# An adaLN transformer block on one core: the rebuilt end of the program against the plain one

## The chip, the cores and the metric

The kernel runs on one core of one Trainium2 chip. A core has TensorE (PE, matrix products into PSUM), VectorE (DVE), ScalarE (ACT), GpSimd (POOL) and SyncE (SP), which here issues nearly all DMA transfers. Each engine works through its own queue in order; semaphores tie the queues together. The metric is the device time of the whole program in microseconds: the median of several runs. The profile is one execution of the same program.

## The reference

One block of a transformer with adaptive layer norm, on 8 sequences of 1024 tokens, width 512, 16 heads of 32, hidden width 2048, all in f32:

```python
mod = silu(condition) @ Wada + bada
sh_a, sc_a, gt_a, sh_m, sc_m, gt_m = split(mod, 6)
xm = layernorm(x, g1, be1) * (1 + sc_a) + sh_a
x  = x + gt_a * (causal_attention(xm, Wqkv) @ Wproj + bproj)     # softmax over the keys
xm = layernorm(x, g2, be2) * (1 + sc_m) + sh_m
x  = x + gt_m * (gelu(xm @ W1 + b1) @ W2 + b2)
```

The second layer norm needs a token's whole projected row, and the projection needs all 16 heads of that token. So behind the last attention group there is a fixed order: quotient, projection, residual, layer norm, MLP, store.

## The kernel before, in words

**Tiling.** The tokens are cut into 16 blocks of 512 (`NB`), two for each sequence; block n is the first or second half of its sequence. Widths are cut into chunks of 128 (`NC` = 4 for 512). The 16 heads are worked in 4 groups of 4 heads, because four heads of 32 fill 128 partitions. A block is also four tiles of 128 tokens (`NTT`).

**Two streams.** `attend` walks over blocks and groups and issues the attention: for each unit of keys the transposed scores (`weights_T`, line 1456), ACT's exponential into a tile `pT` (L1479, one of three slots), POOL's causal mask for diagonal units (L1484), the product with the values (`weigh`, L1507), and the running sum of the exponentials over the units, by which the output is divided at the end (L1608, L1611). A group of a second-half block has seven units: four of 512 keys by queries, then the diagonal ones of 512, 384 + 128 and 256. Unit 0's `pT` is the accumulator and units 1 to 6 are added to it, four heads each. A slot comes free when its addition and its product are done, so the exponential of unit k waits for the addition of unit k - 2. Everything else (q, k, v, projection, MLP: "linear work") is a generator that yields before each product. PE gets pieces of it between the attention's steps. MLP and projections use Strassen-like schemes with seven products of half size, whose operands are sums such as T3, T4 or `combine`d parts of the hidden tile hT.

**The planner.** The order is written out at build time. `now` holds each engine's planned time, `written` and `left` when a value is there and when its reader is done. `note` adds the cost of each issued instruction. `work` advances the linear thread that can go on soonest, `step_aside` lets linear work go ahead while an attention step would wait. `jobs` are DVE pieces (reciprocals, statistics of the layer norm) that are issued when DVE's planned time isn't ahead of PE's; `pool_jobs` likewise for POOL. `either` puts a two-operand operation on POOL (planned 120 + 2.28 n ns for n elements a partition) or on DVE (60 + 1.24 n), with a margin in favour of POOL:

```python
if max(now["DVE"], t) + on_dve + margin[0] < max(now["POOL"], t) + on_pool:
```

The margin is 1500 ns until `attend` has returned, and 0 from there to the end (L1680).

**A group's end.** `finish` (L1525 on) sums the accumulator over partitions by a product with ones, copies the sums (`rec`) and the outputs (`top`) out on ACT, inverts `rec` in four quarters on DVE (L1540) and multiplies; the result goes into qT's chunk g, which has been used up, and is called `attT` in the projection.
- For most groups the multiplication is one 128x512 operation on POOL (L1557). For group 2 of the last block it is on DVE (L1554).
- For the last group of all, each quarter is multiplied on DVE straight after its reciprocal (L1547) and marked as ready by itself.
- In the last group of all, the additions for heads 1 and 3 are on DVE (L1608), those for heads 0 and 2 on POOL (L1611).

**The projection** (`project_out`, L201 for its products) has 4 chunks for each of 4 tiles. Its result is gated (`y`, L193), added to the residual `xr`, and the bias `gba` is added by pool jobs. For the last block the chunks 0 to 2 of tiles 0 and 1 are issued ahead of the last group's quotient, the chunk 3 of a tile waits for its quarter alone, and each tile is followed by its residual addition (L927) and its own layer norm on DVE and ACT (`normalize_tile`, L596 to L608). Other blocks add to the residual through `either` and normalize all four tiles together (`normalize`, L555 to L580). Then `modulated` transposes on PE (L641) and scales.

**The down projection** (`down`) has four parts. `settle` gates a quarter of the result and adds it to the residual, both through `either` (L158 on DVE, L161 on POOL); `store` writes two tiles out (L988). For the last block the last product is made in two halves of 128 tokens (`last_product`): each half has its own two DVE operations of 128x256 (L1058, L1059) and its own store (L1063).

While the last group of block 15 is worked, the linear work left is the second half of block 14's down projection. It settles the quarters `v_d`, `p_d` and `y_d`.

Of the kernel before, what the change touches and what calls it, by code (L numbers as in the profile page):

```python
# [9 lines left out]
F32 = mybir.dt.float32  # L10
# [12 lines left out]
def kernel(  # L23
# [33 lines left out]
    nc = tc.nc  # L57
# [90 lines left out]
    margin = [1500]  # L148

    def either(out, a, b, op, reads, writes):  # L150

        n = 1
        for d in out.shape[1:]:
            n *= d
        on_dve, on_pool = 60 + 1.24 * n, 120 + 2.28 * n
        t = due(reads, writes)
        if max(now["DVE"], t) + on_dve + margin[0] < max(now["POOL"], t) + on_pool:
            nc.vector.tensor_tensor(out, a, b, op)  # L158
            note("DVE", on_dve, reads, writes, port=True)
# [430 lines left out]
    def normalize_tile(xt, key, t, source):  # L590

        mv = small.tile([P, 2], F32, tag="mv1", name=f"mv_{key}_{t}")
        rstd = small.tile([P, 1], F32, tag="rstd1", name=f"rstd_{key}_{t}")
        offset = small.tile([P, 1], F32, tag="offset1", name=f"offset_{key}_{t}")
        st = small.tile([P, nc.vector.BN_STATS_DIM], F32, tag="st", name=f"st_{key}_{t}")
        nc.vector.bn_stats(st, xt)  # L596
        nc.vector.bn_aggr(mv, st)  # L597
        note("DVE", 850, [source], [("mv", key, t)])
        nc.scalar.activation(rstd, mv[:, 1:2], AF.Sqrt, bias=eps)  # L599
        note_act(300, "sqrt", [("mv", key, t)], [("rstd", key, t)])  # L600
        written["hat", key, t] = NEVER

        def apply():
            nc.vector.reciprocal(rstd, rstd)  # L604
            nc.vector.scalar_tensor_tensor(offset, mv[:, 0:1], -1.0, rstd, ALU.mult, ALU.mult)  # L605
            note("DVE", 360, [("rstd", key, t)], [("rstd", key, t)], port=True)
            xh = tmp.tile([P, D], F32, tag="hat", name=f"xh_{key}_{t}", bufs=NTT)
            nc.scalar.activation(xh, xt, AF.Identity, bias=offset, scale=rstd)  # L608
            note_act(800, None, [("rstd", key, t)], [("hat", key, t)])
            hats.setdefault(key, []).append(xh)  # L610

        return apply

# [52 lines left out]
    def accumulate(pairs, reads=(), close=True):  # L666
        yield reads, [BANK]
        bank = lin_bank()
        for i, (lhsT, rhs) in enumerate(pairs):
            if i:  # L670
                yield [], []
            matmul(banks[bank], lhsT, rhs, i == 0, close and i == len(pairs) - 1, reads, bank)
        return bank
# [213 lines left out]
    def project_out(n):  # L887
        at = take(NC)
        yield [("attended", n)], []
        attT = qTs[n]  # L890
# [16 lines left out]

        for t, xt in enumerate(tiles):
            if last:
                while len(begun) <= max(t, 1):  # L910
                    yield from begin(len(begun))
                bank = begun[t]
                yield [("att", n, t)], []
                matmul(
                    banks[bank], attT[:, NC - 1, ts(t, P)], piece(at[NC - 1]), False, True,
                    [("att", n, t)], bank,
                )
            else:
                bank = yield from accumulate(
                    [(attT[:, c, ts(t, P)], piece(at[c])) for c in range(NC)], [("att", n)]  # L920
                )
# [69 lines left out]
    def down(n, part):  # L991
# [41 lines left out]
        def last_product(u3, next_pieces):  # L1033

            kh, tokens = places["B21"]
            c = half(1, HB)
            gate = gate_rows["gm"][:, c]
            xr = residual[n]
            b, h = blocks[n]
            for m in range(2):  # L1040
                nc.vector.tensor_tensor(u3[:, m, :], u3[:, m, :], gate, ALU.mult)
                nc.vector.tensor_tensor(xr[:, m, c], xr[:, m, c], u3[:, m, :], ALU.add)
                note("DVE", 800, [key("u3")], [("xr", n, m)])
            for m in range(2):
                yield [(n, "B21")], [BANK]
                bank = lin_bank()
                for i in range(NQ):
                    for k in range(2):
                        if i + k:
                            yield [], []  # L1050
                        at_q = 2 * i + k
                        hT = hTs[n, 2 * kh + at_q // NC][:, at_q % NC, tokens]
                        matmul(
                            banks[bank][:, :HB], hT[:, ts(m, P)], halves(next_pieces[i])[:, k, :],
                            at_q == 0, at_q == 2 * NQ - 1, [(n, "B21")], bank,
                        )
                y = tmp.tile([P, HB], F32, tag="y", name=f"y_last_{m}")
                nc.vector.tensor_tensor(y, banks[bank][:, :HB], gate, ALU.mult)  # L1058
                nc.vector.tensor_tensor(xr[:, m, c], xr[:, m, c], y, ALU.add)  # L1059
                note("DVE", 800, [("l", bank)], [("xr", n, m)])  # L1060
                live[bank] = False
                r0 = h * TB + m * P
                nc.sync.dma_start(out[b, r0 : r0 + P, :], xr[:, m, :])  # L1063
            release(*next_pieces)

# [38 lines left out]
        else:  # L1104
# [412 lines left out]
    def finish(n, g):  # L1517
# [25 lines left out]
        if (n, g) == groups[-1]:  # L1543
            for i in range(NTT):
                invert(i)
                some = slice(i * part, (i + 1) * part)
                nc.vector.tensor_tensor(qTs[n][:, g, some], top[:, some], rec[:, some], ALU.mult)  # L1547
                note("DVE", 200, [kr, "top"], [("att", n, i)])
            return

        def quotient():
            invert(3)
            if n == NB - 1 and g == NC - 2:
                nc.vector.tensor_tensor(qTs[n][:, g, :], top, rec, ALU.mult)  # L1554
                note("DVE", 700, [kr, "top"], [("att", n)], port=True)
            else:
                nc.gpsimd.tensor_tensor(qTs[n][:, g, :], top, rec, ALU.mult)  # L1557
# [8 lines left out]
    def attend():  # L1566
        previous = None
        for n in range(NB):
# [21 lines left out]
            for g, k, upto in slots:  # L1590
# [9 lines left out]
                if k > 0:  # L1600
                    acc, first = totals[n, g]
                    for _, c0, w in parts:
                        for j in range(HPG):
                            into = acc[:, j, TB - w :]
                            keys = [("p", slot)], [("acc", n, g), ("p", first)]
                            if j % 2 and (n, g) == groups[-1]:

                                nc.vector.tensor_tensor(into, into, pT[:, j, c0 : c0 + w], ALU.add)  # L1608
                                note("DVE", 150 + 2 * w, *keys, port=True)
                            else:  # L1610
                                nc.gpsimd.tensor_tensor(into, into, pT[:, j, c0 : c0 + w], ALU.add)  # L1611
                                note("POOL", 230 + 2.07 * w, *keys)
# [67 lines left out]
    margin[0] = 0  # L1680
    run_excursions()
    run_jobs(True)
    written["attended", NB - 1] = 0.0
# [51 lines left out]
```

## Time and profile before

| | |
|---|---|
| median of 3 runs | 3650.88 us (3647.89 to 3653.37) |
| the profiled execution | 3647.89 us, its span 3646.2 us |
| mean granted TensorE clock | 0.995 |
| PE busy | 3571.6 us, 98% |
| DVE, POOL, ACT busy | 2179.1, 2014.6, 1329.2 us |
| last addition of the last group | ends at 3520.46 us of the span |
| first product of the last block's MLP | 3545.10 us |
| PE's last product | ends at 3642.13 us |

How to read the lines below: in a timeline a line gives start, duration, engine, line of the kernel, operation, output and inputs, shapes, count, and in brackets how long the engine had been idle before and what released it. `bank` are the three PSUM banks of the linear work. In the windows a line gives the stretch, its length, the busy time of PE, PEld, DVE, ACT and POOL with the number of instructions, then the granted clock, the DMA share and GB/s.

### The profile page before, as it was taken

What the parts mean: (1) busy time and instruction counts of PE and PEld (TensorE: products, weight loads), DVE (VectorE), ACT (ScalarE), POOL (GpSimd) and SP (SyncE); (2) the same over time, 40 slices, a digit from 0 to 9 for tenths busy, and PEclk for the clock granted to TensorE, in tenths of its full rate; (3) what the DMA queues carried; (4) which work ended last, traced back from release to release, by engine and by line L of the source; (5) the groups of instructions that cost most, each with busy time, mean ns of one, the idle gap of its engine ahead of it and who ended that gap; (6) DMA issues with size and microseconds to landing.
All of it is one profiled execution on the core that took longest, in us unless ns stands there. A gap on an engine that the chain in (4) does not pass through costs nothing. (4 is left out here: it accounts for less than half of the span.)

```text
span 3646.2 us, 121167 instructions
## 1 busy us (share of the span) xinstructions
PE 3571.6 (98%) x54821; PEld 1770.1 (49%) x54821; DVE 2179.1 (60%) x2501; ACT 1329.2 (36%) x1413; POOL 2014.6 (55%) x2039
## 2 busy tenths in 40 slices
PE   8999999999999999999999999999999999999999
PEld 4434445445554455544545444454544545445445
DVE  6766675564746557465564656746667465664663
ACT  2335234252333523335242352424524244241431
POOL 3656645656455664566636665456654566544560
PEclk9999999999999999999999999999999999999999
DMA  6623333333333343433434334343333433334334
GB/s 220 225 92 104 104 103 109 123 106 119 114 115 112 106 126 111 134 94 104 126 106 143 91 100 123 106 137 103 97 122 110 140 100 103 117 97 143 92 107 138
DMA packets 307894, 430.35 MB, mean 118 GB/s; under 512 B 25900, under 2 KB 176236, under 8 KB 307380
## 3 DMA queue, kind: packets, MB, share of 16 engines
q1 hardware_dynamic: 307264, 422.56, 37.9%
q8 instruction: 432, 7.08, 0.8%
q14 instruction: 82, 0.67, 0.1%
q10 hardware_dynamic: 116, 0.03, 0.0%
HBM read 394.12 MB, written 28.38 MB: 116 GB/s over the span
## 5 line engine op out<-in xcount | busy, mean ns | idle before, releaser
L1611 POOL TENSOR_TENSOR pT<-pT,pT 128x512 f32<-128x512 f32 (+3 forms) x1266 | 1189.2, 973 | 524.9 <-ACT pT L1479 377.1
L1479 ACT ACTIVATE pT<-st 128x2048 f32<-128x2048 f32 (+1 forms) x320 | 546.5, 1708 | 951.3 <-PE st L1467 909.0
L201 PE MATMUL bank<-w,hT 128*32 128x256 f32 x14336 | 808.6, 380 | 2.8 <-DVE hT L1006 2.1
L1392 DVE TENSOR_REDUCE mx<-sc 128x4 f32<-128x1024 f32 (+3 forms) x381 | 664.4, 1757 | 192.4 <-PE sc L1372 185.8
L201 PEld LDWEIGHTS bank<-w,hT 128*32 128x32 f32 x14336 | 452.1, 110 | 354.0 <-issue 58.0
L201 PE MATMUL bank<-xm_m,w 128*32 128x256 f32 x8192 | 506.6, 380 | 0.6 <-ACT rec L1531 0.5
L1484 POOL TENSOR_SCALAR_AFFINE_SELECT pT<-pT 128x512 f32<-128x512 f32 x256 | 175.3, 696 | 576.9 <-ACT pT L1479 576.9
L201 PE MATMUL bank<-t_m,w 128*32 128x256 f32 x6144 | 383.2, 380 | 0.9 <-ACT hT L188 0.9
L201 PEld LDWEIGHTS bank<-xm_m,w 128*32 128x32 f32 x8192 | 253.3, 110 | 252.0 <-issue 98.0
L1456 PE MATMUL st<-qT,kT 32*128 32x512 f32 (+3 forms) x3072 | 339.6, 526 | 21.0 <-DVE mx L1392 20.0
L1372 PE MATMUL sc<-kT,qT 32*128 32x256 f32 (+3 forms) x3048 | 340.6, 527 | 2.9 <-DVE mx L1392 1.9
L1384 DVE TENSOR_TENSOR sc<-sc,mask 128x1024 f32<-128x1024 f32 (+1 forms) x191 | 166.7, 873 | 248.5 <-PE sc L1372 225.5
L1507 PE MATMUL po<-pT,v 128*32 128x512 f32 (+3 forms) x3072 | 312.7, 493 | 2.2 <-POOL pT L1484 1.2
L201 PEld LDWEIGHTS bank<-t_m,w 128*32 128x32 f32 x6144 | 191.9, 110 | 175.7 <-issue 54.2
L201 PE MATMUL bank<-xm_a,w 128*32 128x256 f32 x3968 | 243.5, 381 | 0.0
L201 PE MATMUL bank<-w,qT 128*32 128x512 f32 x2048 | 241.1, 597 | 0.4 <-DVE qT L1547 0.2
L1540 DVE RECIPROCAL rec<-rec 128x128 f32<-128x128 f32 x256 | 224.6, 919 | 8.5 <-ACT rec L1531 8.5
L1456 PEld LDWEIGHTS st<-qT,kT 32*128 32x128 f32 x3072 | 128.9, 184 | 182.7 <-issue 57.5
L1372 PEld LDWEIGHTS sc<-kT,qT 32*128 32x128 f32 x3048 | 126.8, 184 | 161.0 <-ACT pT L1479 77.4
L193 DVE TENSOR_TENSOR hT<-bank,u_u 128x512 f32<-128x512 f32 x192 | 130.2, 686 | 120.9 <-PE bank L201 116.7
L201 PE MATMUL bank<-t_a,w 128*32 128x256 f32 x2944 | 187.2, 382 | 0.0
L1479 ACT ACT_TABLE_LOAD x89 | 114.2, 1283 | 189.3 <-PE st L1467 188.6
(205 smaller groups left out, 3589.5 us busy)
## 6 DMA issues: line engine op xcount, KB each, us to landing
w<-in_L_cond_W_dram SPq DMA_DIRECT2D x384, 256.0 KB, 2.9
w<-kept_up_S SPq DMA_DIRECT2D x256, 256.0 KB, 2.6
w<-kept_down_S SPq DMA_DIRECT2D x256, 256.0 KB, 2.7
w<-kept_qkv_S SPq DMA_DIRECT2D x180, 256.0 KB, 3.0
w<-in_L_cond_Wqkv_dram SPq DMA_DIRECT2D x147, 256.0 KB, 3.3
hat<-in_x_dram SPq DMA_DIRECT2D x64, 256.0 KB, 3.2
w<-in_L_cond_Wproj_dram SPq DMA_DIRECT2D x64, 256.0 KB, 3.8
xr<-in_x_dram SPq DMA_DIRECT2D x64, 256.0 KB, 4.2
```

Source lines behind the costliest of these rows:

```text
L193: nc.vector.tensor_tensor(out, src, other, op)
L201: nc.tensor.matmul(ps[r, :], lhsT[:, r], rhs, start=start, stop=stop, skip_group_check=True)
L1372: nc.tensor.matmul(sc[:, j, c0 : c0 + w], qTs[n][r, g, ts(qt, P)], keys_of(n, kh)[r, g, :w], start=True, stop=True, skip_group_check=True,)
L1384: nc.vector.tensor_tensor(diagonal, diagonal, mask[:, :span].unsqueeze(1).to_broadcast([P, HPG, span]), ALU.add,)
L1392: nc.vector.tensor_reduce(mx[:, kh, qt, :], sc[:, :, c0 : c0 + w], axis=AX.X, op=ALU.max)
L1456: nc.tensor.matmul(st[:, j, c0 : c0 + w], kT[r, g, ts(k % NTT, P)], qT[r, g, TB - w :], start=(c0 == 0), stop=False, skip_group_check=True,)
L1479: nc.scalar.activation(pT[:, :, :used], st[:, :, :used], AF.Exp, scale=scale)
L1484: nc.gpsimd.affine_select(diagonal, diagonal, pattern=[[0, HPG], [1, P]], compare_op=ALU.is_ge, fill=0.0, base=0, channel_multiplier=-1,)
L1507: nc.tensor.matmul(po[r, TB - w :], v[:, k % NTT, g * P + j * hd : g * P + (j + 1) * hd], pT[:, j, c0 : c0 + w], start=(k == 0), stop=last ...
L1540: nc.vector.reciprocal(some, some)
L1611: nc.gpsimd.tensor_tensor(into, into, pT[:, j, c0 : c0 + w], ALU.add)
```

## The change

The last group, the last projection and the last down projection are treated like all others. The additions of the last group are all on POOL. The quotient of group 2 of the last block is on POOL. The last quotient is one operation on POOL behind four reciprocals. The projection of the last block begins when that quotient has been issued, tile after tile with all four chunks. The residual additions go through `either` and the four tiles are normalized together behind the last of them. The margin of `either` stays 1500 ns to the end. The last product of the down projection is one product of 256 tokens, added to `u3`, settled through `either` and stored with two transfers. The gated results `y` of the last projection lie in four buffers in place of two.

```diff
-    margin = [1500]
...
-        if max(now["DVE"], t) + on_dve + margin[0] < max(now["POOL"], t) + on_pool:
+        if max(now["DVE"], t) + on_dve + 1500 < max(now["POOL"], t) + on_pool:
...
-    def normalize_tile(xt, key, t, source):
...
-    def accumulate(pairs, reads=(), close=True):
+    def accumulate(pairs, reads=()):
...
     def project_out(n):
...
-        last = n == NB - 1
-        if last:
-            for t in range(NTT):
-                written["att", n, t] = NEVER
-        begun = []
-
-        def begin(t):
-
+        for t, xt in enumerate(tiles):
             bank = yield from accumulate(
-                [(attT[:, c, ts(t, P)], piece(at[c])) for c in range(NC - 1)], [("att", n)], False
+                [(attT[:, c, ts(t, P)], piece(at[c])) for c in range(NC)], [("att", n)]
             )
-            begun.append(bank)
-
-        for t, xt in enumerate(tiles):
-            if last:
-                while len(begun) <= max(t, 1):
-                    yield from begin(len(begun))
-                bank = begun[t]
-                yield [("att", n, t)], []
-                matmul(
-                    banks[bank], attT[:, NC - 1, ts(t, P)], piece(at[NC - 1]), False, True,
-                    [("att", n, t)], bank,
-                )
...
-            y = tmp.tile([P, D], F32, tag="y", name=f"y_{n}_{t}", bufs=2)
-            ky = y_key("proj", True)
+            tag, bufs = ("hat", NTT) if n == NB - 1 else ("y", 2)
+            y = tmp.tile([P, D], F32, tag=tag, name=f"y_{n}_{t}", bufs=bufs)
+            ky = ("y", n, t) if n == NB - 1 else y_key("proj", True)
             combine_out(y, bank, banks[bank], gate_rows["ga"], [("row", "ga")], [ky], ALU.mult)
-            if last:
-                run_pool_jobs(True)
-                nc.vector.tensor_tensor(xt, xt, y, ALU.add)
-                note("DVE", 700, [ky, ("xr", n, t)], [("xr", n, t)], port=True)
-                following = normalize_tile(xt, f"m{n}", t, ("xr", n, t))
-                if t > 0:
-                    pending()
-                pending = following
-            else:
-                add_to(xt, y, [ky], [("xr", n, t)])
-        if last:
-            pending()
+            add_to(xt, y, [ky], [("xr", n, t)])
         release(*at)
         run_pool_jobs(True)
-        if not last:
-            normalize(tiles, f"m{n}", [("xr", n, t) for t in range(NTT)])
+        normalize(tiles, f"m{n}", [("xr", n, t) for t in range(NTT)])
...
-        def last_product(u3, next_pieces):
...
-            if n == NB - 1:
-                yield from last_product(u3, next_pieces=[next(at) for _ in range(NQ)])
-                return
             bank, ps = yield from product("B21")
...
-        if (n, g) == groups[-1]:
-            for i in range(NTT):
-                invert(i)
-                some = slice(i * part, (i + 1) * part)
-                nc.vector.tensor_tensor(qTs[n][:, g, some], top[:, some], rec[:, some], ALU.mult)
-                note("DVE", 200, [kr, "top"], [("att", n, i)])
-            return
-
         def quotient():
             invert(3)
-            if n == NB - 1 and g == NC - 2:
-                nc.vector.tensor_tensor(qTs[n][:, g, :], top, rec, ALU.mult)
-                note("DVE", 700, [kr, "top"], [("att", n)], port=True)
-            else:
-                nc.gpsimd.tensor_tensor(qTs[n][:, g, :], top, rec, ALU.mult)
-                note("POOL", 1285, [kr, "top"], [("att", n)])
+            nc.gpsimd.tensor_tensor(qTs[n][:, g, :], top, rec, ALU.mult)
+            note("POOL", 1285, [kr, "top"], [("att", n)])
...
-                            if j % 2 and (n, g) == groups[-1]:
-
-                                nc.vector.tensor_tensor(into, into, pT[:, j, c0 : c0 + w], ALU.add)
-                                note("DVE", 150 + 2 * w, *keys, port=True)
-                            else:
-                                nc.gpsimd.tensor_tensor(into, into, pT[:, j, c0 : c0 + w], ALU.add)
-                                note("POOL", 230 + 2.07 * w, *keys)
+                            nc.gpsimd.tensor_tensor(into, into, pT[:, j, c0 : c0 + w], ALU.add)
+                            note("POOL", 230 + 2.07 * w, [("p", slot)], [("acc", n, g), ("p", first)])
...
     open_unit = attend()
     alone[0] = True
-    margin[0] = 0
     run_excursions()
-    run_jobs(True)
-    written["attended", NB - 1] = 0.0
     close(*open_unit)
```

More of the change, by code (lines that the diff above doesn't have):

```diff
@@ L588, in normalize @@
             add_job(lambda t=t: statistics(t), [sources[t]], key[0] == "m")
-    def normalize_tile(xt, key, t, source):
[L592 to L612, printed above, removed]
     def modulated(key, gain, shift, b, guards):
@@ L671, in accumulate @@
                 yield [], []
-            matmul(banks[bank], lhsT, rhs, i == 0, close and i == len(pairs) - 1, reads, bank)
+            matmul(banks[bank], lhsT, rhs, i == 0, i == len(pairs) - 1, reads, bank)
         return bank
@@ L889, in project_out @@
         yield [("attended", n)], []
-        attT = qTs[n]
+        attT = qTs.pop(n)
         tiles = [residual[n][:, t, :] for t in range(NTT)]
@@ L908, in project_out @@
-        for t, xt in enumerate(tiles):
-            if last:
-                while len(begun) <= max(t, 1):
-                    yield from begin(len(begun))
-                bank = begun[t]
-                yield [("att", n, t)], []
-                matmul(
-                    banks[bank], attT[:, NC - 1, ts(t, P)], piece(at[NC - 1]), False, True,
-                    [("att", n, t)], bank,
-                )
-            else:
-                bank = yield from accumulate(
-                    [(attT[:, c, ts(t, P)], piece(at[c])) for c in range(NC)], [("att", n)]
-                )
-            y = tmp.tile([P, D], F32, tag="y", name=f"y_{n}_{t}", bufs=2)
-            ky = y_key("proj", True)
-            combine_out(y, bank, banks[bank], gate_rows["ga"], [("row", "ga")], [ky], ALU.mult)
-            if last:
-                run_pool_jobs(True)
-                nc.vector.tensor_tensor(xt, xt, y, ALU.add)
-                note("DVE", 700, [ky, ("xr", n, t)], [("xr", n, t)], port=True)
-                following = normalize_tile(xt, f"m{n}", t, ("xr", n, t))
-                if t > 0:
-                    pending()
-                pending = following
-            else:
-                add_to(xt, y, [ky], [("xr", n, t)])
@@ L1031, in product @@
             return bank, banks[bank].rearrange("p (i n) -> p i n", n=HB)
-        def last_product(u3, next_pieces):
[L1035 to L1064, printed above, removed]
         def stage(kind, tag, bufs=1):
@@ L1604, in attend @@
                             into = acc[:, j, TB - w :]
-                            keys = [("p", slot)], [("acc", n, g), ("p", first)]
-                            if j % 2 and (n, g) == groups[-1]:
-                                nc.vector.tensor_tensor(into, into, pT[:, j, c0 : c0 + w], ALU.add)
-                                note("DVE", 150 + 2 * w, *keys, port=True)
-                            else:
-                                nc.gpsimd.tensor_tensor(into, into, pT[:, j, c0 : c0 + w], ALU.add)
-                                note("POOL", 230 + 2.07 * w, *keys)
+                            nc.gpsimd.tensor_tensor(into, into, pT[:, j, c0 : c0 + w], ALU.add)
+                            note("POOL", 230 + 2.07 * w, [("p", slot)], [("acc", n, g), ("p", first)])
                 previous = (n, g, parts, pT, slot, k == n_slots - 1)
```

## The prediction

> **What bounds the kernel now.** I read the page first, then the chain that ended last, then the last 160 us engine by engine in order of time, and then an earlier stretch of the same loop for undisturbed prices. The page:
>
> ```profile
> PE 3571.6 (98%) x54821; PEld 1770.1 (49%) x54821; DVE 2179.1 (60%) x2501; ACT 1329.2 (36%) x1413; POOL 2014.6 (55%) x2039
> ```
>
> PE is the bound nearly everywhere, so an edit counts only where PE waits. All edits sit behind one point, the first partial-sum addition of the last group (block 15, group 3) at 3491.6 us: up to there the two programs issue the same instructions in the same order. PE's own waits behind it stand in the timelines of PE and POOL:
>
> ```profile
> 3515.91 2.34 PE L201 MATMUL bank<-w,hT 128*32 128x256 f32 x40
> 3519.82 1.31 PE L1525 MATMUL bank<-pT,ones 128*32 128x512 f32 x6 [1.57 <-POOL pT L1611]
> 3526.96 9.12 PE L201 MATMUL bank<-w,qT 128*32 128x512 f32 x80 [0.25 <-DVE qT L1547]
> 3542.14 3.04 PE L641 MATMUL bank<-ident,xh_m 128*128 128x128 f32 x13 [0.23 <-ACT xh_m L608]
> 3545.10 2.01 PE L201 MATMUL bank<-xm_m,w 128*32 128x256 f32 x32
> ...
> 3506.31 3.46 POOL L1611 TENSOR_TENSOR pT<-pT,pT 128x512 f32<-128x512 f32 x2
> 3519.06 1.40 POOL L1611 TENSOR_TENSOR pT<-pT,pT 128x256 f32<-128x256 f32 x2
> ```
>
> PE runs without a hole to 3518.25, waits for POOL's last addition (3519.06 + 1.40 = 3520.46), projects until 3526.96 + 9.12 = 3536.08, and gets its first MLP product at 3545.10. Between 3545.10 and 3642.13 it is full again. So three stretches can be priced: up to POOL's last addition (I call its end T, now 3520.46), T to the first MLP product (now 24.64 us), and the tail behind PE's end at 3642.13. POOL has no gap over 0.1 us from 3491.6 to T, though half of the heads are added on DVE.
>
> Undisturbed prices come from an earlier group of the same shape, where POOL adds all four heads (timeline of POOL), and from the tail:
>
> ```profile
> 3056.31 4.99 POOL L1611 TENSOR_TENSOR pT<-pT,pT 128x512 f32<-128x512 f32 x4
> 3064.31 5.55 POOL L1611 TENSOR_TENSOR pT<-pT,pT 128x384 f32<-128x384 f32 x8
> 3070.54 2.80 POOL L1611 TENSOR_TENSOR pT<-pT,pT 128x256 f32<-128x256 f32 x4
> 3098.19 1.28 POOL L1557 TENSOR_TENSOR qT<-top,rec 128x512 f32<-128x512 f32 x1
> ...
> 3642.16 0.43 DVE L1058 TENSOR_TENSOR y_last<-bank,row_gm 128x256 f32<-128x256 f32 x1 [1.65 <-PE bank L201]
> 3642.62 0.42 DVE L1059 TENSOR_TENSOR xr<-xr,y_last 128x256 f32<-128x256 f32 x1
> ```
>
> A group's unit costs POOL 5.0 us for four 512-wide heads; before, two heads took 3.46 beside DVE's two.
>
> **The change, stretch 1: additions of the last group and the quotient of the one before it.** DVE's half of the additions goes to POOL. From 3491.61 POOL has units 1 to 3 at 4.99 (14.97), unit 4 with its mask at 0.72 + 4.99, unit 5 with two masks at 1.19 + 5.55, unit 6 with its mask at 0.75 + 2.80: 30.97 us. The quotient of group 2 comes back from DVE, 1.28 and 0.03 of gap; its reciprocals now find DVE free, so it is issued behind unit 1's additions and stands in this queue. Sum 32.3. In the same stretch lie the eight SBUF operations that finish block 14's last quarters (three on v_d, three on p_d, two on y_d). The first six ran on POOL at about 1.3 to 1.6. The planner moves one to DVE when POOL's planned end is more than 695 + 1500 - 1287 = 908 ns behind the operands. POOL will be nearly 5 us behind when v_d is ready (u_d ends at 3498.0, units 1 and 2 with the quotient end near 3502.9) and further behind for p_d and y_d, so I put all eight on DVE. There they hinder POOL: four additions took 6.33 us at 3442.17 beside three DVE operations, 1.34 more than 4.99, so 0.45 for each DVE operation. Eight cost 3.6. T becomes 3491.6 + 32.3 + 3.6 = 3527.5: 7.0 us later. Bounds: no hindrance, 3.4 later; all eight left on POOL, where the six of v_d and p_d stand ahead of the last additions at 1.28 and 0.07 of gap (8.1 in place of 3.6, the two of y_d behind them), 11.6 later. I take the value between, since the 0.45 comes from three rows that agree (3506.31 gives 0.48, 3520.42 gives 0.45).
>
> On this the Trainium skill (SBUF — State Buffer, section Who interferes with whom) says that the port pair of DVE and GpSimd is a whole-instruction lock, so that the loser blocks fully. By that each DVE operation of 0.69 us would cost POOL 0.69, T would be another 1.9 us later and the forecast 3668; the rows with 0.45 decide.
>
> The PE work of the stretch is unchanged; it runs out some 5 us before T, and what fills that gap in the new order is nothing.
>
> **Stretch 2: T to the first MLP product.** Removed: the quotient by quarters, two tiles begun on their first three chunks, and the tile-wise layer norm. New chain, by rows of this trace: 0.1 to the ones product, 1.04 for it (3487.20), 0.14 and ACT's copy 0.59 (3488.38), 0.1 and four reciprocals 3.38 (3159.39, x4), 0.08 and POOL's quotient 1.28, 0.1, then PE. Only tile 0's first three chunks are done by then, so 13 of 16 chunk products follow, 0.86 each (60 records, 7.5 products, in 6.62 at 3529.46): 11.2. So far 18.0. Behind it: last y 0.72; statistics of four tiles, all issued behind it, 0.81 apart (3143.13 to 3143.95): 3.25; the last residual addition, now POOL's 1.28, is hidden by the first three of them. Root, reciprocal and offset with gaps 0.1 + 0.30 + 0.05 + 0.38, four normalizations on ACT 2.92 (3162.89, x4), 0.05; the last 13 transposes 3.0 as now. That is 10.8, and 28.8 against 24.64: 4.2 later.
>
> PE's clock adds to it. The windows:
>
> ```profile
> 3538.00:3539.00 1.00, 0.15 (x1) 0.16 (x1) 0.90 (x2) 0.79 (x2) 0.00 (x0) 0.74 0.53 177
> 3539.00:3540.00 1.00, 0.32 (x1) 0.03 (x1) 0.97 (x2) 0.00 (x0) 0.00 (x0) 0.50 0.04 13
> 3545.00:3547.00 2.00, 2.00 (x37) 1.11 (x40) 0.95 (x3) 0.91 (x2) 0.21 (x1) 0.92 0.00 0
> ```
>
> The granted clock (third column from the end) halves some 2.4 us after PE's last long run and is back 3 us after work resumes. PE would idle about 5 us before the last weighing, so the ones product runs at half clock: 1.0 more. A second idle of some 2.6 us stands before the quotient lands. Its cost lies between 0 and 1.5 (three microseconds at half clock); I take 0.7. Stretch 2 is 5.9 later. The Trainium skill (TensorE: Matmul & The Clock Gate, Part 1) puts the idle window at about 3.4 us, free-running; by it the second idle would cost nothing and the forecast would be 3665.3. The 2.4 us of the row are nearer to the idle, so I keep 0.7.
>
> The four gate-bias additions move from beside DVE's chain to POOL behind the quotient, 5.1 us within the 11.2 of projection; with the four residual additions POOL has 10.3 there and is free for the last one. If that cover went, 1.3 would show.
>
> **Stretch 3: the MLP and the tail.** With the margin at 1500 again, combinations of hT go to POOL (about 2.8 each) in place of DVE. B11 is done near 5.6 us after 3617.5 and B21 5.6 behind it, needed at 3628 and 3635: free; without that slack each would cost its overrun. T3 on POOL and T4 on DVE are needed 7 us on, free. The last product now ends all at once: y 0.69, gate and residual on POOL 1.31 and 1.33 with gaps 0.2, so 3.5 behind PE against 3642.62 + 0.42 - 3642.13 = 0.9: 2.6 later. Then SP issues two 256 KB stores back to back instead of one that was left over: one issue of 0.4 at least, one transfer of 0.7 more at most; 0.6. Tail 3.2 later. No other queue of SP moves: the weight loads wait on the same releases.
>
> **Sum.** 7.0 + 5.9 + 3.2 = 16.1 us on the profiled execution: span 3646.2 to 3662.3, its time 3647.89 (1.7 around the span) to 3664.0. The median of the runs stands 3.0 above it, so 3650.88 + 16.1, about 3667.
>
> **The rivals.**
> (a) POOL isn't hindered by DVE and PE's clock holds. For it: PE has small jobs in the gap. Against: three contended rows. T 3.4, stretch 2 4.2, tail 3.2: 10.8 later, 3661.7.
> (b) The planner leaves those eight operations on POOL. T 11.6, the rest as above: 20.7, 3671.6. Against: the backlog worked out above.
> (c) The end hardly matters, within 7.3 us (0.2%, about what a measurement of this kernel can tell). It needs T unmoved, stretch 2 at 4.2 and tail 3.0: 7.2, 3658.1. For it: POOL loses six operations of 1.3 to 1.6 us. Against: POOL's additions and masks alone end at 3522.6.
> (d) Faster, by relief of the shared port alone: in the last group POOL and DVE each run long beside each other (POOL 1.73 for a 512-wide head against 1.25), and the change ends that. It decides from T earlier than 3520.46 - 4.2 - 3.2 = 3513.1, so POOL would have to finish in 21.5 us what its rows price at 31.0. By those it ends in (a); were it true with T at 3512, the time would be 3649.8.
>
> **How the numbers follow.** Main case 0.62 (its own range +13 to +19.5, 3664 to 3670.5), (a) 0.18, (b) 0.13, (c) 0.05, (d) 0.02. The range takes (a) to (b) in, with 2.5 to 3.4 us for the spread of the runs shown (3647.89 to 3653.37): 3659 to 3675. Faster 0.02, same 0.05, slower 0.93.
>
> **What would show it.** POOL's line for the additions holds all four heads, its last end near 3527.5; v_d, p_d and y_d operations on DVE inside that stretch; a ones product of about 2 us; 13 chunk products behind one POOL quotient; first MLP product near 3558; behind PE's end two POOL operations of 1.3. Wrong if T comes before 3523, if statistics run between the tiles, or if the four normalizations start before the projection ends; and wrong altogether if PE shows holes inside the 97 us of the MLP, where I cost the margin's change at nothing.

## The result and the profile after

The changed kernel takes 3665.73 us (median of 5 runs, 3662.55 to 3667.84) against 3650.88 us: +14.9 us, a ratio of 1.0040 with a 95% interval of 1.0026 to 1.0055. Run once more beside other kernels it took 3664.88 against 3649.32 us, +15.6, a ratio of 1.0041 (1.0027 to 1.0055). The forecast was 3667.

The profiled execution took 3667.59 us with a span of 3665.9. The last group on POOL, from its timeline:

```profile
3494.01 4.96 POOL L1497 TENSOR_TENSOR pT<-pT,pT 128x512 f32<-128x512 f32 x4 [2.05 <-ACT pT L1383]
3498.92 1.74 POOL L1449 TENSOR_TENSOR qT<-top,rec 128x512 f32<-128x512 f32 x1
...
3512.10 6.40 POOL L1497 TENSOR_TENSOR pT<-pT,pT 128x512 f32<-128x512 f32 x4
...
3519.65 6.39 POOL L1497 TENSOR_TENSOR pT<-pT,pT 128x384 f32<-128x384 f32 x8
...
3526.71 2.77 POOL L1497 TENSOR_TENSOR pT<-pT,pT 128x256 f32<-128x256 f32 x4
```

All four heads are on POOL, group 2's quotient stands behind unit 1, and POOL is busy from the first addition at 3494.01 to the last one's end at 3529.48. Unit 4 takes 6.40 us in place of the undisturbed 4.99, for DVE works beside it (timeline of DVE):

```profile
3512.79 1.65 DVE L156 TENSOR_TENSOR p_d<-p_d,row_gm 128x512 f32<-128x512 f32 x1
3514.47 1.65 DVE L156 TENSOR_TENSOR xr<-xr,p_d 128x512 f32<-128x512 f32 x1
```

v_d, p_d and y_d are all on DVE. PE waits in the places that the forecast named (timeline of PE):

```profile
3526.68 1.08 PE L1411 MATMUL po<-pT,v 128*32 128x256 f32 x8 [5.90 <-POOL pT L1388]
3527.54 3.06 PE L1429 MATMUL bank<-pT,ones 128*32 128x512 f32 x6
...
3537.28 13.06 PE L199 MATMUL bank<-w,qT 128*32 128x512 f32 x104 [3.09 <-POOL qT L1449]
...
3558.11 3.04 PE L615 MATMUL bank<-ident,xh_m 128*128 128x128 f32 x13 [0.23 <-ACT xh_m L578]
3561.07 2.54 PE L199 MATMUL bank<-xm_m,w 128*32 128x256 f32 x32
```

The windows show the granted clock (third column from the end) at half behind the first wait, and again behind the one for the quotient:

```profile
3522.00:3524.00 2.00, 0.00 (x0) 0.00 (x0) 1.97 (x2) 0.00 (x0) 2.00 (x3) 1.00 0.35 125
3526.00:3528.00 2.00, 1.32 (x9) 0.43 (x10) 0.00 (x0) 0.00 (x0) 1.92 (x4) 0.50 0.38 152
3538.00:3540.00 2.00, 2.00 (x16) 0.57 (x12) 0.69 (x1) 0.00 (x0) 2.00 (x2) 0.62 0.00 0
```

And the tail is one operation on DVE and two on POOL:

```profile
3658.66 0.69 DVE L191 TENSOR_TENSOR y_d<-bank,u_d 128x512 f32<-128x512 f32 x1 [6.21 <-PE bank L199]
3659.43 1.26 POOL L159 TENSOR_TENSOR y_d<-y_d,row_gm 128x512 f32<-128x512 f32 x1 [2.87 <-DVE y_d L191]
3660.77 1.26 POOL L159 TENSOR_TENSOR xr<-xr,y_d 128x512 f32<-128x512 f32 x1
```

Everything behind the first addition of the last group (S) can be cut into five stretches: to the end of the last addition (T), the end of the last projection (E), the first MLP product (U), the end of PE's last product (M) and the end of the span. Each number is a difference of two times of that kernel's timeline, in us. The runs below are in the table too.

| kernel | S | S to T | T to E | E to U | U to M | M to end | S to end |
|---|---|---|---|---|---|---|---|
| before | 3491.61 | 28.85 | 15.62 | 9.02 | 96.98 | 4.12 | 154.6 |
| changed | 3494.01 | 35.47 | 20.86 | 10.73 | 97.51 | 7.32 | 171.9 |
| changed, again | 3493.63 | 35.53 | 19.16 | 10.70 | 96.90 | 7.28 | 169.6 |
| additions on POOL alone | 3490.20 | 35.52 | 13.06 | 9.03 | 97.56 | 4.13 | 159.3 |
| changed, additions split | 3492.39 | 28.85 | 18.27 | 10.74 | 97.15 | 7.30 | 162.3 |
| tail alone | 3490.25 | 28.85 | 14.84 | 8.11 | 96.93 | 7.32 | 156.1 |
| changed, PE kept busy | 3493.16 | 35.49 | 18.06 | 11.17 | 97.09 | 7.23 | 169.0 |
| changed, settling left out | 3490.90 | 31.90 | 19.78 | 10.75 | 96.90 | 7.27 | 166.6 |
| changed, settling on POOL | 3493.86 | 42.15 | 19.17 | 10.74 | 96.94 | 7.24 | 176.2 |
| norm together alone | 3491.59 | 28.86 | 15.64 | 10.81 | 97.80 | 4.10 | 157.2 |
| quotient whole alone | 3494.51 | 28.87 | 20.85 | 6.57 | 97.85 | 4.05 | 158.2 |
| best end | 3490.31 | 25.35 | 17.28 | 9.66 | 97.06 | 4.04 | 153.4 |
| best end 2 | 3489.93 | 25.36 | 16.48 | 10.21 | 97.05 | 4.07 | 153.2 |

S itself differs by up to 4.6 us, though the same instructions run before it; what is known of that comes in the last section. The stretches behind it are what the edits act on: +17.3 and +15.0 us in the two profiles of the changed kernel. Each row is one execution. Of the four runs that make one part of the change alone, only the one with the whole quotient has a time that lies clear of the kernel before, by its interval; what the others cost is read from the stretches.

### The profile page after: what moved, and what is told of

Same layout as the page of the kernel before. It is cut to its first block, busy times and chain, and to the rows that moved or that the text cites. A ratio compares the mean times of both kernels' runs of the same rounds, so it can differ in the third digit from the quotient of the medians.

```text
span 3665.9 us, 121141 instructions
## 1 busy us (share of the span) xinstructions
PE 3578.9 (98%) x54821; PEld 1770.8 (48%) x54821; DVE 2157.1 (59%) x2466; ACT 1328.1 (36%) x1410; POOL 2039.3 (56%) x2060
## 4 chain that ended last, share of the span: by engine, by line
PE 87%; DVE 7%; POOL 2%; ACT 2%; issue 2%; DMA 0%; SPq 0%; ACTq 0%; POOLq 0%; DVEq 0%
PE bank L199 59%; PE st L1360 8%; PE sc L1276 8%; PE po L1411 7%; DVE mx L1296 2%; PE st L1371 2%; PE bank L1429 2%; POOL pT L1497 2%; PE bank L615 1%; DVE hT L946 1%; DVE sc L1288 1%; DVE xr L156 1%; ACT pT L1383 1%; DVE t_m L156 1%; PE bank L1334 0%
## 5 line engine op out<-in xcount | busy, mean ns | idle before, releaser
L1497 POOL TENSOR_TENSOR pT<-pT,pT 128x512 f32<-128x512 f32 (+3 forms) x1280 | 1202.8, 974 | 525.7 <-ACT pT L1383 377.9
L1444 DVE RECIPROCAL rec<-rec 128x128 f32<-128x128 f32 x256 | 224.1, 918 | 16.1 <-ACT rec L1435 16.1
```

The source lines that it names most:

```text
L1444: nc.vector.reciprocal(some, some)
```

## The experiments

**One part alone: the additions on POOL.**

```diff
-                            if j % 2 and (n, g) == groups[-1]:
...
+                            nc.gpsimd.tensor_tensor(into, into, pT[:, j, c0 : c0 + w], ALU.add)
...
-            if n == NB - 1 and g == NC - 2:
-                nc.vector.tensor_tensor(qTs[n][:, g, :], top, rec, ALU.mult)
```

> The kernel before with one part of the change alone: all four heads of the last group added on POOL, and group 2's quotient on POOL. Theory (POOL is the chain there): POOL's stretch from the first addition to the last one's end grows from 28.85 us to about 35.5, v_d and p_d move to DVE, PE idles 5 to 6 us ahead of the last weighing and the ones product runs at half clock; stretch 2 (last addition to first MLP product) stays near 24.6 plus 1; +7 to +8 us in all. Rival (the additions are slack, the loss of the change lies in its later chain): the stretch grows by under 3 us and the time by under 3.

3651.69 against 3649.54 us, a ratio of 1.0007 (0.9998 to 1.0016). POOL's stretch grows as the theory said, 28.85 to 35.52, but T to E falls from 15.62 to 13.06, so 4.7 us are left in the stretches, not 7 to 8. PE's timeline, then DVE's, say why:

```profile
3516.80 5.33 PE L201 MATMUL bank<-w,qT 128*32 128x512 f32 x48
3522.92 0.64 PE L1507 MATMUL po<-pT,v 128*32 128x256 f32 x8 [0.78 <-POOL pT L1484]
```

```profile
3517.85 1.46 DVE L158 TENSOR_TENSOR y_d<-y_d,row_gm 128x512 f32<-128x512 f32 x1
...
3527.54 0.95 DVE L1540 RECIPROCAL rec<-rec 128x128 f32<-128x128 f32 x1 [6.81 <-ACT rec L1531]
```

With the projection of the kernel before, PE fills the wait for POOL with the six chunk products of two tiles that are begun ahead, and y_d is settled while DVE has nothing else. In the kernel before both lie behind T. PE waits 0.78 us ahead of the last weighing, not 5 to 6, and the last ones product ends 1.1 us behind T, where it ends 2.0 behind it in the changed kernel: the clock did not halve here, against what was expected. So a later T is worth its full length only when nothing can be done ahead of it.

**The changed kernel with the additions split again.** The same lines the other way round.

> The changed kernel with that same part undone: heads 1 and 3 of the last group on DVE again, group 2's quotient on DVE again, all else as changed. Theory: POOL's stretch is back near 29 us, no long idle of PE ahead of the last weighing, so the ones product runs at full clock; stretch 2 is some 30.5 (31.6 measured in the changed kernel less 1.0), the tail is unchanged; 7 to 8 us under the changed kernel, 7 to 9 over the one before. Rival (later chain alone): under 3 us below the changed kernel.

3656.74 us, +7.2, ratio 1.0021 (1.0011 to 1.0031); the changed kernel is 14.9 and 15.6 above the one before, so this is some 8 us under it, as the theory said. The ones product is at full clock (PE waits 1.58 us ahead of it; in the changed kernel it waits 5.90 ahead of the last weighing), and so are the 13 chunk products behind the quotient (timeline of PE):

```profile
3528.14 11.37 PE L199 MATMUL bank<-w,qT 128*32 128x512 f32 x104 [3.22 <-POOL qT L1453]
```

T to E is 18.27 and E to U 10.74 where the forecast's rows gave 18.0 and 10.8. The rest of the change alone costs 7.7 us in the stretches. The additions cost 7.3 to 9.6 us on top of it against 4.7 alone; the 9.6 has 1.7 in it from the half clock behind the quotient, which this run did not meet.

**One part alone: the margin and the tail.**

```diff
-            if n == NB - 1:
-                yield from last_product(u3, next_pieces=[next(at) for _ in range(NQ)])
-                return
...
-    margin[0] = 0
```

> The kernel before with the end of the change alone: the margin stays 1500 ns and the last product is one product, settled through the planner and stored with two transfers. Theory as in the prediction: tail 3.2 us longer (PE's last product to the end of the span 7.3 in place of 4.1), nothing else, +3.2. Rival: the margin also acts ahead of the last reciprocals. With it at 0, y_d's gate and residual (2.7 us with contention) stand on DVE in front of the four reciprocals; with 1500 they go to POOL, the reciprocals start some 2.5 us sooner, stretch 2 falls from 24.6 to about 22.5, and the sum is +1.

3651.56 us, ratio 1.0003 (0.9994 to 1.0013); in the stretches +1.5: the rival. M to the end is 7.32 in place of 4.12, the 3.2 of the forecast. But T to U falls from 24.64 to 22.95, because y_d's two operations have left the front of the reciprocals (timeline of POOL, then of DVE):

```profile
3520.51 1.28 POOL L161 TENSOR_TENSOR y_d<-y_d,row_gm 128x512 f32<-128x512 f32 x1 [1.41 <-DVE y_d L193]
```

```profile
3520.90 0.95 DVE L1537 RECIPROCAL rec<-rec 128x128 f32<-128x128 f32 x1 [0.47 <-ACT rec L1528]
```

In the kernel before, y_d stands on DVE ahead of that reciprocal (timeline of DVE, before):

```profile
3523.97 1.65 DVE L158 TENSOR_TENSOR xr<-xr,y_d 128x512 f32<-128x512 f32 x1
3525.55 0.94 DVE L1540 RECIPROCAL rec<-rec 128x128 f32<-128x128 f32 x1
```

There the reciprocal starts 5.1 us behind T, here 1.8. The end of the kernel before was thus not at its best: with the margin at 0 already there, it loses 1.7 us.

**PE kept busy in its three waits.**

```diff
+        if last_wait[0]:
+            keep_busy(22, "weigh")
...
+                    if c == NC - 1:
+                        keep_busy(8, "quotient")
...
+        if key == f"m{NB - 1}":
+            keep_busy(20, "hats")
```

`keep_busy` issues products of bf16 constants of 512 columns into the score tile, which nobody reads.

> The changed kernel with bf16 products of constants, read by nobody, issued in PE's three waits: 22 ahead of the last weighing, 8 ahead of the product that waits for the last quotient, 20 ahead of the transposes of the last layer norm. Nothing else is changed. Theory (half clock after idling): granted clock 1.0 through these stretches; ones product 2.0 to 1.0, the 13 chunk products 13.06 to about 11.3, the last 13 transposes 3.04 to under 2, the first MLP product 2.54 to 1.9; 4 to 5 us less in all. Rival (those lengths come from data that arrives late, not from the clock): the same lengths, no gain.

3664.32 us, ratio 1.0042 (1.0027 to 1.0057); the time doesn't tell it from the changed kernel. From S to the end it takes 169.0 us in place of 171.9 and 169.6, so 2.9 and 0.6 less, not 4 to 5. In the stretches: T to the copy of the sums on ACT takes 1.1 us in place of 2.0, and the 13 chunk products 11.37 in place of 13.06 (timeline of PE):

```profile
3535.34 11.37 PE L199 MATMUL bank<-w,qT 128*32 128x512 f32 x104 [1.19 <-POOL qT L1474]
3546.64 4.49 PE L868 MATMUL busy_hats<-mcols,minus_ones 128*128 128x512 bf16 x19
...
3554.92 3.04 PE L618 MATMUL bank<-ident,xh_m 128*128 128x128 f32 x13 [0.38 <-ACT xh_m L579]
```

The window over the last transposes has the clock at half (third column from the end):

```profile
3555.00:3556.00 1.00, 1.00 (x5) 1.00 (x6) 0.57 (x1) 0.00 (x0) 0.00 (x0) 0.50 0.00 0
```

So the first two lengths were the clock's, and the third part failed: the filling ended 3.8 us before the last transposes, the three single transposes in between did not hold the clock, and the 13 still took 3.04. The run of the changed kernel beside the best end tells the rest.

> The changed kernel once more, beside the best version: POOL's stretch 35.5, stretch 2 31.6, tail 7.3, and the time 14 to 17 us above the kernel before; against the kernel with PE kept busy (14.8 above) it tells whether that one's 2.9 us in the stretches are seen in the time.

There the wait for the quotient was 2.94 us and the 13 products took 11.37 with no filling, at full clock:

```profile
3538.00:3540.00 2.00, 2.00 (x26) 0.54 (x19) 0.69 (x1) 0.00 (x0) 2.00 (x3) 1.00 0.00 0
```

The second wait halves the clock in some executions and not in others, so one filled run doesn't show that filling gains there. What is left to it is the 0.9 of the first wait, which took 2.0 us from T to the copy in both profiles of the changed kernel.

**DVE beside POOL: the eight operations left out, and forced onto POOL.**

```diff
+            special[0] = n == NB - 2
             add_to(v3, u2, [key("u2")], [key("v3")])
             settle(n, 0, 1, v3, key("v3"))
+            special[0] = False
```

The same brackets stand around p_d's and y_d's. In the first run `either` skips the DVE instruction while `special` is set and plans its time, in the second it takes POOL.

> The changed kernel without the eight SBUF operations on DVE that finish block 14's last quarters (three on v_d, three on p_d, two on y_d); the plan keeps their time, so nothing else moves, and three quarters of block 14 lack their last terms. What is left is POOL's queue without DVE beside it. Theory (0.45 us of hindrance for each): POOL's stretch from the first addition to the last one's end falls from 35.47 to about 32, that is 31.0 of additions and masks and 1.3 of quotient. Rival (the port is a lock held for whole instructions, 0.69 for each at least): it falls by 5.5 to under 30. Rival (no hindrance, POOL's rows are long for another cause): it stays at 35.5.

One execution, 3659.22 us. The stretch is 31.90, 3.6 us shorter: 0.45 for each of the eight, and the units have their undisturbed lengths again (timeline of POOL).

```profile
3497.05 9.94 POOL L1506 TENSOR_TENSOR pT<-pT,pT 128x512 f32<-128x512 f32 x8
...
3507.67 5.00 POOL L1506 TENSOR_TENSOR pT<-pT,pT 128x512 f32<-128x512 f32 x4
...
3513.81 5.53 POOL L1506 TENSOR_TENSOR pT<-pT,pT 128x384 f32<-128x384 f32 x8
```

> The changed kernel with those eight operations forced onto POOL, which is the prediction's case (b). Theory: POOL's stretch is 31.0 + 1.3 + six operations of 1.35, about 40.4, against 35.5; y_d's two stand behind the last addition and are hidden by the reciprocals; PE idles longer, stretch 2 stays at 31.6; 5 us more in all. Rival (DVE's hindrance costs as much as the operations on POOL): 35 to 36.5.

One execution, 3671.86 us. Against 40.4 expected the stretch is 42.15. The miss is the place of y_d (timeline of POOL):

```profile
3530.67 1.27 POOL L161 TENSOR_TENSOR y_d<-y_d,row_gm 128x512 f32<-128x512 f32 x1
...
3533.24 2.77 POOL L1505 TENSOR_TENSOR pT<-pT,pT 128x256 f32<-128x256 f32 x4
```

It stands ahead of the last additions; presumably the planner, with POOL so late, ran all the linear work before it issued them, but the runs don't show why. Each operation costs POOL about 1.3 there (10.25 us for the eight, against the run without them) and 0.45 on DVE; the choice of DVE shortens POOL's stretch by 6.6 us.

**The two halves of the second stretch.** Norm together: tile-wise `normalize_tile` gives way to `normalize` behind the last tile.

```diff
-                nc.vector.tensor_tensor(xt, xt, y, ALU.add)
...
-                following = normalize_tile(xt, f"m{n}", t, ("xr", n, t))
...
+                nc.gpsimd.tensor_tensor(xt, xt, y, ALU.add)
...
-        if not last:
+        if True:
             normalize(tiles, f"m{n}", [("xr", n, t) for t in range(NTT)])
```

> The kernel before with one half of stretch 2 alone: the residual additions of the last projection on POOL and its four tiles normalized together behind the last; quotient by quarters and tiles begun ahead as before. Theory, by the prediction's rows: projection ends 15.6 us behind the last addition as before, 10.8 from there to the first MLP product in place of 9.0: stretch 2 is 26.4 in place of 24.6, +1.8. Rival (the four layer norms tile by tile gain nothing, since they queue up on DVE): 24 to 25, no change.

3650.54 against 3648.89 us, ratio 1.0004 (0.9995 to 1.0013). T to U is 26.45, +1.8, as expected.

Quotient whole: the branch of `finish` for the last group and the tiles begun ahead are taken out, and `attended` is no longer set ahead of the last weighing.

```diff
-        if (n, g) == groups[-1]:
-            for i in range(NTT):
-                invert(i)
...
-                while len(begun) <= max(t, 1):
-                    yield from begin(len(begun))
...
-    run_jobs(True)
-    written["attended", NB - 1] = 0.0
     close(*open_unit)
```

> The kernel before with the other half of stretch 2 alone: the last quotient is one operation on POOL behind four reciprocals and no tile of the projection is begun ahead; tile-wise layer norm on DVE as before. Theory: the projection ends 18.0 us behind the last addition in place of 15.6, but DVE then has its 2.6 us for each tile hidden behind PE's 3.4, so 6.9 follow in place of 9.0: stretch 2 is about 25, less than 1 us longer, some 2 more where y_d stands ahead of the reciprocals or the clock halves. Only both halves together give the 29.0 of the split-addition run. Rival (the quotient's loss adds up whatever the layer norm does): 27 and more.

3653.54 us, ratio 1.0012 (1.0002 to 1.0021). E to U is 6.57, so the tile-wise norm does hide behind the slower projection. But T to E is 20.85, not 18.0: the reciprocals start 2.7 us behind T in place of 2.0, for y_d stands ahead of them, and the products behind the quotient ran at half clock (timeline of PE):

```profile
3531.17 13.06 PE L201 MATMUL bank<-w,qT 128*32 128x512 f32 x104 [4.11 <-POOL qT L1539]
```

T to U is 27.42 and on the rival's side of the line. With 11.37 for those products it would be 25.7. The halves cost 1.8 and 1.1 to 2.8 us alone and 4.4 together (29.01 in the run with split additions), all against the kernel before. But the run with split additions also has the margin at 1500, which keeps y_d off DVE there. Against the run with the tail alone, which has it too (22.95), both halves together cost 6.1, and in all 6.2 from S to the end. By that they cost more together than apart; what each costs alone with the margin at 1500 wasn't measured, and there is one profile of each.

**Two tries for a better end.** Four edits to the kernel before; the second try takes back the third and moves the first behind the projection.

```diff
     close(*open_unit)
+    margin[0] = 0
...
+            if n == NB - 2:
+                pool_jobs.append((settled, [key("u3")]))
...
+                    nc.gpsimd.tensor_tensor(xt, xt, y, ALU.add)
...
+                if key == f"m{NB - 1}" and c == 0:
+                    keep_busy((4, 6, 6, 1)[t], f"hat_{t}")
```

> The kernel before with four edits at its end: the margin goes to 0 behind the last weighing instead of ahead of it, so that y_d is settled on POOL and doesn't stand in front of the last reciprocals; p_d is settled behind the last additions instead of ahead of them; tiles 0 to 2 of the last projection are added to the residual on POOL, tile 3 on DVE; products of constants are issued on PE between the first transposes of the last layer norm. Theory: T comes up to 1.5 us sooner for PE, stretch 2 loses 1.7 by the first edit, 0.8 by the third, 1.3 by the fourth (13 transposes 3.04 to 1.7); 4 to 6 us under the kernel before. Rival (the last chain is bound by DVE all the same, and the products of constants stand in the way of the transposes): within 2 us of it.

3646.28 against 3649.32 us, ratio 0.9992 (0.9983 to 1.0000).

> The best end so far without two of its faults: residual additions of the last projection all on DVE again (each tile's statistics stood 1.5 us behind POOL's addition), and the margin goes to 0 only behind the last projection, so that y_d is on POOL and not ahead of tile 0's gating. Kept: p_d behind the last additions, products of constants between the first transposes. Theory: first MLP product 2 to 3 us sooner than in that run (its 52.3 us behind the first addition fall to about 50), 5 to 6 us under the kernel before, 0.15%. Rival (DVE's chain of four tiles takes the gain back): 3 us under it as before.

3647.46 against 3648.89 us, ratio 0.9996 (0.9987 to 1.0005). Neither can be told from the kernel before with certainty. In the stretches both gain 1.2 to 1.4 us, not 4 to 6. POOL ends 3.5 us sooner, but PE still has linear work then, and DVE's four tiles bound the rest: in the first try three of them wait 1.46 us each for POOL's residual addition, in the second all stand behind two gate-bias additions that the planner put on DVE (3.08 us). What did work is the filling between the transposes (timeline of PE, second try):

```profile
3540.16 1.89 PE L643 MATMUL bank<-ident,xh_m 128*128 128x128 f32 x13 [0.16 <-ACT xh_m L608]
```

13 transposes take 1.89 in place of 3.04 us where the clock is held (1.00 in the windows from 3534 to 3544).

## Why the prediction was right

**Stretch 1** was forecast 7.0 us longer; it is 6.6 and 6.7. The sum of POOL's undisturbed units and the quotient, 32.3, was measured by itself as 31.9, the hindrance by DVE, 3.6, as 3.6. The planner's choice of DVE for all eight operations came as worked out from its backlog. The whole-instruction lock that the Trainium skill states (SBUF — State Buffer, section Who interferes with whom) would, as an estimate from 0.69 each, make it 5.5 us for the eight; these runs show 0.45 for each, not 0.69. (Two side sums of the working are wrong by 1 us: 1.9 above 3667 is 3669, not 3668, and 0.7 below it is 3666.3, not 3665.3. The forecast doesn't rest on them.)

**Stretch 2** was forecast 5.9 us longer, 4.2 by the chain and 1.7 by the clock; it is 6.95 and 5.2. The chain's own rows held: 18.27 and 10.74 where the clock was full against 18.0 and 10.8 (a chunk product is 0.87, not 0.86: the working's own row gives 6.62 / 7.5 = 0.88). Two of the four gate-bias additions ran on DVE behind the reciprocals, where the working had all four on POOL; the quotient beside them took 1.49 in place of 1.28. The 1.0 for the ones product was 0.9. The 0.7 for the second wait was a mean of a thing that is 0 or 1.7: 1.7 in the first profile, 0 in the second. The bound of 1.5 was a little low. So neither of the two profiles shows the 5.9, and that it lies between them is to that extent luck.

**Stretch 3** was forecast 3.2 longer, and is 3.2 (7.32 and 7.28 against 4.12): 2.5 for the operations and 0.7 for the stores behind them, forecast as 2.6 and 0.6. The margin's change in the MLP cost nothing, as said: U to M is 96.9 where the first product has full clock, as in the second profile, and the 97.51 of the first has a first product of 2.54 us in place of 1.93.

**The sum.** 16.1 us stood against 17.3 and 15.0 in the stretches and 14.9 and 15.6 by the medians. For the profiled execution the working had 3664.0, and it took 3667.59; 2.4 us of the difference lie ahead of S, where the working expected none.

**Rivals.** (a), no hindrance and full clock, fell with the eight operations left out and with the filled waits. (b) did not occur; forced, it costs 6.6, of which the text had only 4.5, since it put y_d behind the last additions. (c) and (d) needed POOL faster than its rows.

**What the working had not seen.** It priced the changed kernel as a whole, and so the total came out. Asked part by part it would have been wrong. The additions alone cost 4.7 us in the stretches, not 7 to 8: T to E falls by 2.6, by the chunk products done ahead and by y_d, which these runs don't part, and the clock holds. The tail with its margin costs 1.5, not 3.2, because the kernel before loses 1.7 us by y_d in front of its last reciprocals, which the margin at 1500 gives back. The rebuilt projection and norm then cost 6.2, not 4.2. Taken in this order, the tail 1.5, projection and norm 6.2 and the additions 7.3 to 9.6 make up the 15.0 and 17.3. The sentence that nothing fills PE's gap ahead of T held for the changed kernel alone: it is the missing start of the projection that makes the additions' delay count in full.

## What to carry to other kernels

Where an engine's queue is the chain, price it as a sum of its undisturbed rows, plus the hindrance that a row with the neighbour beside it shows, and work out from the planner's costs which engine the rest will take. A delay in front of a wait costs its full length only if nothing can be issued ahead of that wait, so parts that fill and parts that delay have to be priced together. An operation that nobody waits for does harm when it stands in the queue in front of one that somebody waits for.

## What the runs showed of the hardware

TensorE's clock falls after some short waits and not after others of the same length. The same wait of PE for DVE, ahead of the same instructions in block 15, group 2, is followed by full clock in the kernel before and by half clock in the changed one (the wait and the window behind it, of before):

```profile
3454.89 1.14 PE L1456 MATMUL st<-qT,kT 32*128 32x512 f32 x8 [1.86 <-DVE mx L1392]
```

```profile
3456.00:3458.00 2.00, 2.00 (x35) 0.89 (x32) 0.00 (x0) 1.64 (x1) 0.00 (x0) 1.00 0.00 0
```

And of the changed kernel:

```profile
3455.66 1.26 PE L1360 MATMUL st<-qT,kT 32*128 32x512 f32 x8 [1.87 <-DVE mx L1296]
```

```profile
3456.00:3458.00 2.00, 2.00 (x16) 0.34 (x12) 0.00 (x0) 0.54 (x1) 0.00 (x0) 0.64 0.00 0
```

From that score product to the next such one of 512 columns in the next group, work that is the same in all 13 profiles of the table, PE takes 22.36 to 22.37 us in seven of them and 24.00 to 24.05 in six (both of the changed kernel, the split additions, PE kept busy, settling on POOL, quotient whole). Five of the six are among the six profiles of the changed kernel and its variants, one among the seven of the kernel before and its variants; whether that is chance or something in the programs isn't shown. Waits for the last quotient of 2.80, 2.94 and 3.22 us left the clock full, such of 3.09, 3.25 and 4.11 us halved it, and the 2.94 and the 3.09 are two executions of one program. Waits of 5.66 us and more always did. So a wait of about 1.9 to 3.3 us costs nothing or up to 1.7 us, though the instructions are the same. The Trainium skill (TensorE: Matmul & The Clock Gate, Part 1) says that the gate judges by a window that runs freely, without regard to the program, which fits that; it asks for an idle window of some 3.4 us, and here half clock followed waits of 1.87 us. That the place in the window decides isn't shown by these runs.

This is also where a part of S comes from. The score product behind that wait starts between 3453.22 and 3456.16 in the 13 profiles, and the 1.6 us of the half clock come on top; these 2.9 and 1.6 make up the 4.6 by which S differs. What moves the 2.9 isn't known, nor whether this makes up the 5 us by which runs of one kernel differ.

Three single transposes 0.7 us apart did not hold the clock: 3.8 us behind the filling it was at half. Behind bf16 products of 512 columns it was full wherever these ended up to 1.6 us ahead of the work: at 1.05 and 1.19 us in the run with PE kept busy, at 0.16 to 1.61 between the transposes of the two tries for a better end.
